# Graph attention on one core: factors of the rows in PSUM, scores of the tile two ahead behind the unit's sum

## The chip, the core and the metric

The kernel runs on one NeuronCore of a Trainium2 chip. Five engines work side by side, each in the order of its own queue: PE (matrix products), DVE (vector work), ACT (activation functions and copies), POOL (here: issues the gathers) and SP (issues the other DMAs). They wait for one another through semaphores. SBUF is the working memory of 128 partitions; [...] The metric is the time of one execution in microseconds (us); the median of several runs counts.

## The reference, cut to what matters

Two layers stand one after the other, each with a residual and a layer norm. Layer 0 is one graph attention of 8 heads over a graph of 4096 nodes with 512 features; layer 1 is an attention of 8 heads, then one of a single head of 512, then two dense layers. An attention is

```
Wh   = einsum('nf,kfp->knp', x, W)            # projection, 8 heads of 64
e    = leaky_relu(f2[:, :, None] + f1[:, None, :], 0.2)
e    = where(adj > 0, e, -1e16)
att  = softmax(e, axis=-1)                    # over a node's neighbours
out  = einsum('knm,kmp->knp', att, Wh)
```

and layer 0 is `x = layernorm(x + attention(x))`. The adjacency is sparse and skewed: low-numbered nodes have many neighbours.

## The kernel before, in words

A first stage finds every node's neighbours from the adjacency, packs them into lists of 128 edges (chunks), and projects x into a table in HBM. After that come two layers of 8 heads (`heads_layer`, called for `st0` and `st1`), and at the end the layer of one head with the dense layers. This case is about `heads_layer`.

**Tiles and units.** The 4096 nodes are 32 tiles of 128. Tile 0, whose nodes have neighbours nearly everywhere, is worked densely and spread over the whole layer (class `First`). The other 31 tiles go through their edge lists. A tile's chunks are cut into units of at most 6 chunks; a layer has 56 units, and a loop `for i, u in enumerate(units)` writes out the order of the work by hand (`manual_schedule`): each engine executes its share in just the order in which the loop names it. High and low tiles alternate, so that in the middle of the layer a tile of one unit is followed by a tile of two. A tile's first unit has `u.first` set.

**What a unit does.** `gather` (L1349, POOL) brings each chunk's 128 rows of the table to SBUF, five units ahead (`GB = 5` buffers `g`); a row has 8 heads of 64 values and, per head, one more number, the destination's part of the score. `scores` (L1441 to L1446) adds the source's part `s`, applies the leaky ReLU and writes z; ACT puts exp(z), the factor for the denominator, into the row itself (L1446). `powers` (L1455) has ACT write the same exponentials as `wp`, the factors, one number per chunk and head. `scale` first builds 0/1 matrices `sm` that tell which node an edge belongs to (L1506), then multiplies the rows by the factors (L1525, DVE, 128 x 512 numbers per chunk, here called the product). `sum` (L1547, PE) adds up the edges of each node in PSUM (`acc`). The call `weights` is `scores` and `powers` in one.

**After a tile.** Once a tile's sums are complete, `divide` divides by the denominator (L1554, L1566), adds the residual and starts the layer norm (layer 0) or the ELU (layer 1); its rest is L1671 to L1674, or L1657. Then `norm` transposes the result on PE (`pt`, L714), `project` makes the next layer's projection (`ph`, L726), `rows` copies it out on ACT (L753, L760) and writes the table, and `split` cuts the source's scores into three bf16 parts on DVE (L766 on). One step is taken per unit, so that a tile goes through them over some four units. `divide` is done early (`held`) in units that add for tile 0.

**Scores of the source.** Edges need their node's score `s`, which `Attention.spread` brings about for the tile two ahead: PE multiplies 0/1 matrices by the three bf16 parts into `pss` (L1370, L1377), and DVE collects the three into `s` and a scaled `ls` (L1386, L1398). Before, the matmuls come first in a tile's first unit, and the collection last in it.

**Tile 0.** `First.make` has ACT compute 8 blocks of weights (L1609) and scale the rows of one neighbour tile by a factor per head (L1611); `sort_out` masks the weights on DVE (L1619); `add` sums two tiles on PE (L1633, 32 products recorded as one stretch of 3.7 us); `take` adds that to a total on DVE (L1647). Each is spread over the units.

**PSUM.** `acc` takes four banks (two buffers of two banks), `pss` one, and the three others are a ring with the tag `ph`, for projections, transposes and small products. The factors `wp` lie in SBUF, with two buffers: ACT can write a unit's factors while the unit before still uses its own. A tile in a ring is handed out again once its last reader is done, and whoever writes it next waits for that.

Of the kernel before, what the change touches and what calls it, by code (L numbers as in the profile page):

```python
# [11 lines left out]
F32 = mybir.dt.float32  # L12
# [4 lines left out]
AF = mybir.ActivationFunctionType  # L17
# [5 lines left out]
P = 128  # L23
N = 4096
F = 512
NT = N // P
# [12 lines left out]
HS = 8  # L39
DM = 64  # L40
HN = P // 2
GC = 6
# [518 lines left out]
def sparse_path(  # L561
# [24 lines left out]
    nc = tc.nc  # L586
# [49 lines left out]
    class Stage2:  # L636
        def __init__(self, name, heads, dim, dest_first):
            self.name, self.heads, self.dim, self.dest_first = name, heads, dim, dest_first


            self.row = F + heads if heads > 1 else F + 2
            self.part = HF + heads // 2
            self.wide = HF + heads
            self.table = dram.tile([N + 1, self.row], F32, name=f"table_{name}")
            self.s = lists_.tile([P, NT, heads], F32, name=f"ss_{name}")
            self.s3 = lists_.tile([P, NT, 2, 3, heads], BF16, name=f"s3_{name}")
            self.s_row = None if heads > 1 else const.tile([P, 1, P], F32, name="s_row_1")
            self.rd = const.tile([P, NT, heads], F32, name=f"rd_{name}")
            self.xparts = lists_.tile([P, FC, NT], F32, name=f"xparts_{name}")
# [682 lines left out]
    class Attention:  # L1332


        def __init__(self, st, gp, wk, pacc, ps, sb=None):
            self.st, self.gp, self.wk, self.pacc, self.ps, self.sb = st, gp, wk, pacc, ps, sb
            self.s, self.ls, self.acc, self.seen = {}, {}, {}, {}

        def gather(self, u):
# [18 lines left out]
        def spread(self, t):  # L1358


            st, hs = self.st, self.st.heads
            base, n = parts_of(t)[0].first, sum(p.n for p in parts_of(t))
            for name, of in (("s", self.s), ("ls", self.ls)):
                of[t] = self.sb.tile([P, WIDE, hs], F32, name=f"{name}{hs}", tag=name, bufs=3)[:, :n]

            def scores(p, lo):

                pss = self.ps.tile([P, 20, 3, hs], F32, name="pss")
                m = min(20, p.n - lo)
                nc.tensor.matmul(  # L1370
                    pss[:, :m], ident_b,
                    hole[:, p.first + lo : p.first + lo + m, :, None].to_broadcast([P, m, 3, hs]),
                    start=True, stop=False,
                )
                todo = blocks_in(p, lo, m)
                for block, groups, chunks in todo:
                    nc.tensor.matmul(  # L1377
                        pss[:, chunks].rearrange("p m a h -> p m (a h)"),
                        s1[:, ts(p.at + block, P)],
                        st.s3[:, t, groups].rearrange("p g a h -> p g (a h)"),  # L1380
                        start=False, stop=(block, groups, chunks) == todo[-1],
                    )
                return p.first - base + lo, pss[:, :m]

            def collect(lo, pss):
                nc.vector.tensor_reduce(  # L1386
                    self.s[t][:, lo : lo + pss.shape[1]], pss.rearrange("p m a h -> p m h a"), AX.X, OP.add
                )
# [12 lines left out]

            return rest
# [46 lines left out]
        def powers(self, u):  # L1449
            if u.t == 0:  # L1450
                return
            hs, z = self.st.heads, u.z
            if hs > 1:
                u.wp = self.wk.tile([P, GC, hs], F32, name="wp", bufs=2)
                nc.scalar.activation(u.wp[:, : u.n], z, AF.Exp)  # L1455
            else:
                u.w = self.wk.tile([P, GC, hs], F32, name="w")
                nc.scalar.activation(u.w[:, : u.n], z, AF.Exp)  # L1458
# [119 lines left out]
    class First:  # L1578
# [16 lines left out]
        def make(self, step=0):  # L1595

            b = self.made
            self.step = step
            if b == min(self.summed + DW, NT) or step - self.since[b] < REST:
                return  # L1600
            self.made += 1
            rows = by_head(self.rows[b])
            d = rows[:, :, DM]
            d8 = self.sb.tile([P, HS], F32, name="d8", bufs=2)
            w = self.w[b] = self.sb.tile([P, HS, P], F32, name="w0", bufs=DW)
            nc.scalar.activation(d8, d, AF.Copy, scale=0.8)
            nc.scalar.activation(d, d, AF.Exp, scale=0.2)
            for h in range(HS):
                nc.scalar.activation(w[:, h], self.st.s_row[:, h], AF.Exp, scale=0.8, bias=d8[:, h : h + 1])  # L1609
            for h in range(HS):  # L1610
                nc.scalar.activation(rows[:, h, :DM], rows[:, h, :DM], AF.Copy, scale=rows[:, h, DM : DM + 1])  # L1611

        def sort_out(self):
            b = self.sorted
# [63 lines left out]
    def heads_layer(gp, wk, sb, pp, st, nxt, fetch, finish, clear):  # L1678
# [5 lines left out]
        order = [t for pair in zip(range(NT - 1, NT // 2, -1), many) for t in pair] + [1]  # L1684
        assert sorted(order) == list(range(1, NT))
        units = units_of(order)
        units[-1:] = units[-1].cut(units[-1].n - 2)
        groups = [(1, 1), (2, 6), (8, 8), (16, 8), (24, 8)]
        with tc.tile_pool(name=f"ha_{st.name}", bufs=2, space=PSUM, reuse_waits="tile") as pacc, \
                tc.tile_pool(name=f"hp_{st.name}", bufs=1, space=PSUM, reuse_waits="tile") as one, \  # L1690
                tc.tile_pool(name=f"hq_{st.name}", bufs=3, space=PSUM, reuse_waits="tile") as ps, \
                tc.manual_schedule():
            at = Attention(st, gp, wk, pacc, one, whole)
            extra = {}
            if clear:
                for _ in range(GB):
# [2 lines left out]
            first = First(at, whole, pacc, order[:-1] + [0, 1])  # L1699
# [3 lines left out]
            for t in order[:2]:  # L1703
                extra[t] = fetch(t)
            for _ in range(DW):
                first.make()
                first.sort_out()
            first.add(DW)
            first.take()
# [42 lines left out]
            def run(of):  # L1752

                mine = [way for way in ways if way[0] is of]
                for way in ([w for w in mine if w[1] != 0] or mine)[:1]:
                    ways.remove(way)
                    nxt_ = of(*way[1:])
                    if nxt_:
                        ways.append(nxt_)

            ways, out_, resting = [], set(), None
            for i, u in enumerate(units):
                pos = order.index(u.t)
                spread = None
                if u.first and pos + 2 < NT - 1:
                    spread = at.spread(order[pos + 2])
                    extra[order[pos + 2]] = fetch(order[pos + 2])
                if i + 1 < len(units):
                    at.weights(units[i + 1])
                taken = u.first and first.sorted - first.summed >= min(DB, NT - first.summed) > 0  # L1770
                if i > 0:
                    first.make(i)
                run(rows)
                held = None
                at.scale(u)
                first.take()
                if taken:
                    first.add(DB)
                    held = divide(order[pos - 1]) if pos > 0 else None
                    if first.summed == NT:  # L1780
                        extra[0] = fetch(0, spare())
                        resting = i + 2
                at.sum(u)
                if i + GB < len(units):
                    at.gather(units[i + GB])
                run(project)
                if first.sorted < first.made - 1 or first.made == NT:
                    first.sort_out()
                run(split)
                run(row)  # L1790
                if i == len(units) - 2:
                    assert all(way[0] is split for way in ways)
                    mrow = mean_of_all_but(pp, ps, nxt, u.t)
                run(norm)
                if held:
                    ways.append(held)
                elif u.first and pos > 0:
                    ways.append((divide, order[pos - 1]))
                    run(divide)
                if i == resting:  # L1800
                    ways.append(divide_first())
                if spread:
                    spread()
            assert resting and resting < len(units) - 4
            ways.append((divide, order[-1]))
            while ways:
# [89 lines left out]
    wk = ctx.enter_context(tc.tile_pool(name="lw", bufs=3, reuse_waits="tile"))  # L1896
# [32 lines left out]
    with tc.tile_pool(name="ta", bufs=2, space=PSUM, reuse_waits="tile") as pacc, \  # L1929
# [9 lines left out]
        order = [t for block in blocks for t in block]  # L1939
# [380 lines left out]
```

## Time and profile before

Three runs gave a median of 2035.86 us (2034.43 to 2037.29). The profiled execution took longer, as the table shows.

| What | us |
|---|---|
| median of the runs | 2035.86 |
| profiled execution | 2050.6 |
| its span, first to last instruction | 2048.9 |
| first stage, to the first gather at | 320.0 |
| layer 0, products L1525 | 353.0 to 809.0 |
| layer 1, products L1525 | 847.6 to 1305.3 |
| busy over the span: PE | 1656.7 (81%) |
| DVE | 1361.1 (66%) |
| POOL | 1192.1 (58%) |
| ACT | 902.7 (44%) |

The granted PE clock is 0.907 of full speed over the span. A line of the profile names an engine, a kernel line, the operation, what it writes and reads, and then its count, its busy time and the mean time of one instruction. The waits view names an instruction, what released it, and the total, the number and the longest of such waits. In a timeline the first two numbers are the start from the beginning of the span and the time taken, both in us; what stands in brackets is the idle time of the engine before the instruction, and what ended it. Each fp32 product on PE shows as two records. Shares over the whole span mix stages with different limits, so the layers have to be looked at by themselves. POOL's spans are rough, and the issuing of a DMA isn't counted as busy.

### The profile page before, as it was taken

How to read it: one execution, taken by the hardware profiler on the slowest of the kernel's cores; microseconds unless marked ns; L12 is line 12 of the kernel's file. 1: busy time of each engine (PE TensorE's matmuls, PEld its weight loads, DVE VectorE, ACT ScalarE, POOL GpSimd, SP SyncE). 2: the span in 40 equal slices, each digit the busy share in tenths (PEclk: the TensorE clock that was granted, in tenths of full speed). 3: DMA queues.
4: the chain of work that ended last, by engine and by line, in shares of the span. 5: the costliest groups of instructions: out<-in, count | busy, mean ns of one | idle time of the engine just before them, and what ended most of it. 6: DMA issues, size and time to landing. Idle time of an engine off the chain costs nothing.

```text
span 2048.9 us, 31053 instructions
## 1 busy us (share of the span) xinstructions
PE 1656.7 (81%) x9793; PEld 1214.9 (59%) x9793; DVE 1361.1 (66%) x3527; ACT 902.7 (44%) x3288; POOL 1192.1 (58%) x1337
## 2 busy tenths in 40 slices
PE   5997975888887887378777888658899998988987
PEld 2675654555665655256556665436668776766766
DVE  6686765978888776377666676325565656666665
ACT  5986964654555525166545563112123221212211
POOL 5556566888888781688888868173332545445100
PEclk7999996889899989689989999879999999999998
DMA  8798955666666672555565556263355444345210
GB/s 316 294 343 279 318 180 175 179 196 200 179 214 201 194 218 72 139 152 166 159 168 163 161 138 176 89 205 110 99 149 160 130 129 136 108 134 140 66 42 33
DMA packets 140052, 343.69 MB, mean 168 GB/s; under 512 B 39493, under 2 KB 44621, under 8 KB 132198
## 3 DMA queue, kind: packets, MB, share of 16 engines
q0 software_dynamic: 64064, 180.85, 32.0%
q1 hardware_dynamic: 75814, 160.76, 22.7%
q8 instruction: 80, 1.31, 0.3%
q14 instruction: 94, 0.77, 0.1%
HBM read 332.19 MB, written 42.24 MB: 183 GB/s over the span
## 4 chain that ended last, share of the span: by engine, by line
PE 33%; DVE 20%; issue 16%; POOL 9%; DMA 6%; ACT 6%; another core or an unknown queue 1%; POOLq 0%; DVEq 0%; SPq 0%; ACTq 0%
PE acc L1547 10%; POOL g L1349 8%; PE ph L726 6%; DVE g L1525 6%; DMA g<-table_t,idx 6%; PE px L2051 3%; PE acc L1633 2%; PE px L2059 2%; PE py L2051 2%; PE pz L2051 2%; PE py L2059 1%; DVE sm L1506 1%; DVE w L1619 1%; ACT sg L976 1%
## 5 line engine op out<-in xcount | busy, mean ns | idle before, releaser
L1349 POOL DMA_INDIRECT g<-table_t,idx x774 | 1007.1, 1301 | 555.6 <-issue 214.6
L1547 PE MATMUL acc<-g,sm 128*64 128x260 f32 (+2 forms) x3408 | 510.0, 439 | 253.8 <-DVE g L1525 142.8
L1547 PEld LDWEIGHTS acc<-g,sm 128*64 128x64 f32 x3408 | 281.8, 155 | 433.1 <-DVE g L1525 152.0
L726 PE MATMUL ph<-sw_t,xt 128*128 128x264 f32 (+1 forms) x1536 | 379.6, 399 | 12.5 <-ACT xt L1842 6.0
L726 PEld LDWEIGHTS ph<-sw_t,xt 128*128 128x128 f32 x1536 | 292.1, 195 | 97.4 <-issue 23.8
L1525 DVE TENSOR_TENSOR g<-g,wp 128x3072 f32<-128x3072 f32 (+4 forms) x112 | 292.5, 2611 | 0.0
L717 ACT ACTIVATE xt<-pt 128x128 f32<-128x128 f32 x256 | 67.4, 277 | 276.2 <-PE pt L714 188.2
L1609 ACT ACTIVATE w<-s_row,d 128x128 f32<-128x128 f32 x512 | 156.3, 387 | 0.0
L1633 PE MATMUL acc<-rows,w 128*128 128x65 f32 x1024 | 129.0, 287 | 14.7 <-DVE w L1619 14.7
L1633 PEld LDWEIGHTS acc<-rows,w 128*128 128x128 f32 x1024 | 125.1, 203 | 16.5 <-issue 16.5
L1157 DVE MAX8 cand<-key 128x8 f32<-128x85 f32 (+51 forms) x395 | 99.9, 318 | 47.2 <-PE key L991 47.1
L1611 ACT ACTIVATE rows<-rows 128x64 f32<-128x64 f32 x512 | 128.4, 334 | 0.0
L976 ACT ACTIVATE sg<-raw,value 128x2048 bf16<-128x2048 int32 x60 | 120.1, 2008 | 3.6 <-DMA raw<-in_adj_dram 2.9
L1441 DVE TENSOR_TENSOR z<-s,g 128x16 f32<-128x16 f32 (+5 forms) x160 | 29.9, 201 | 129.2 <-DMA g<-table_t,idx 125.1
L2065 ACT ACTIVATE shid<-shid,sl1b 128x256 f32<-128x256 f32 x112 | 50.5, 500 | 117.0 <-DVE shid L2003 115.2
L1657 DVE SCALAR_TENSOR_TENSOR o<-ex,o 128x512 f32<-128x512 f32 x63 | 43.5, 690 | 63.4 <-ACT ex L1656 50.1
L1666 ACT ACTIVATE rstd<-mv,s_eps 128x1 f32<-128x1 f32 x64 | 19.1, 298 | 150.2 <-DVE mv L1663 143.1
L1619 DVE SCALAR_TENSOR_TENSOR w<-w,mask 128x1024 f32<-128x1024 f32 x64 | 77.4, 1212 | 5.2 <-ACT w L1609 5.2
L753 ACT COPY hrow<-ph 128x260 f32<-128x260 f32 (+3 forms) x130 | 44.1, 369 | 70.8 <-PE ph L726 61.0
L1655 ACT ACTIVATE ex<-o 128x512 f32<-128x512 f32 x63 | 39.8, 631 | 77.6 <-DVE o L1573 57.8
L1446 ACT ACTIVATE g<-z 128x48 f32<-128x48 f32 (+4 forms) x112 | 30.3, 271 | 90.9 <-DVE z L1444 60.0
L1514 DVE TENSOR_SCALAR sm<-iota_n,nl,w 128x64 f32<-128x64 f32 x284 | 68.9, 319 | 0.2 <-ACT w L1458 0.2
(282 smaller groups left out, 2813.4 us busy)
## 6 DMA issues: line engine op xcount, KB each, us to landing
raw<-in_adj_dram SPq DMA_DIRECT2D x60, 1024.0 KB
table_t<-hrow SPq DMA_DIRECT2D x64, 260.0 KB
rows<-table_t SPq DMA_DIRECT2D x64, 260.0 KB
xr<-in_x_dram SPq DMA_DIRECT2D x63, 256.0 KB
g<-table_t,idx POOLq DMA_INDIRECT x774
table_t<-hrow SPq DMA_DIRECT2D x32, 257.0 KB
xr<-sx_d SPq DMA_DIRECT2D x32, 256.0 KB
out_dram<-xr SPq DMA_DIRECT2D x32, 256.0 KB
```

The source lines that it names most:

```text
L726: nc.tensor.matmul(ph[:n], columns(c), st.w[:, c, j], start=(c == 0), stop=(c == FC - 1))
L976: nc.scalar.activation(sg[:, ts(i, w)], raw[:, ts(i, w)], AF.Sign, bias=values["half"])
L1157: nc.vector.max(out=cand[:, at : at + 8], in_=key[:, j - w0_ : j - w0_ + n_])
L1349: nc.gpsimd.indirect_dma_start(out=u.g[:, k, : self.st.row], out_offset=None, in_=self.st.table[:, :], in_offset=bass.IndirectOffsetOnAxis ...
L1514: nc.vector.tensor_scalar(sm[:, at + i], of_g, node[k], u.w[:, k], op0=OP.is_equal, op1=OP.mult)
L1525: nc.vector.tensor_mul(body, body, wp[:, :, None].to_broadcast(body.shape))
L1547: nc.tensor.matmul(out_[g * HN : (g + 1) * HN], sm[:, slot], rows(k), start=start, stop=stop)
L1609: nc.scalar.activation(w[:, h], self.st.s_row[:, h], AF.Exp, scale=0.8, bias=d8[:, h : h + 1])
L1611: nc.scalar.activation(rows[:, h, :DM], rows[:, h, :DM], AF.Copy, scale=rows[:, h, DM : DM + 1])
L1619: nc.vector.scalar_tensor_tensor(w, w, 1.0, mask0[:, self.turns[b], None, :].to_broadcast([P, HS, P]), op0=OP.max, op1=OP.mult)
L1633: nc.tensor.matmul(acc[:, j, k * HD : (k + 1) * HD], w[:, h], rows[:, h * HD : (h + 1) * HD], start=(b == lo and k == 0), stop=(b == hi - ...
L2051: nc.tensor.matmul(out_[:, m], a[:, c, ts(k, P)], b[:, c], start=m == 0 and c == 0, stop=k == ks[-1] and c == 1,)
```

## The change

It touches the two layers of 8 heads in four places.

- `wp` moves from SBUF, with two buffers, to one bank of PSUM, with one buffer. That is the bank that `pss` had.
- `pss` takes its turns in the ring of three banks that projections and transposes use (`tag="ph"`).
- In each unit, `scores` and `powers` are called apart. `run(rows)` comes directly after `scores`; then tile 0's exponentials; then `powers`; then tile 0's scaling of rows, which `make` now hands back as a function.
- `spread` is called after the unit's `sum` and the next gather, before `project`, and its collection directly after `sort_out`, ahead of `split`, `row`, `norm` and `divide`. Before, it was called at the start of the unit and the collection came at the end.

The number of products, activations, DMAs and gathers in a unit stays as it is. Its core as a diff:

```diff
-        def __init__(self, st, gp, wk, pacc, ps, sb=None):
+        def __init__(self, st, gp, wk, pacc, ps, sb=None, one=None):
...
-                pss = self.ps.tile([P, 20, 3, hs], F32, name="pss")
+                pss = self.ps.tile([P, 20, 3, hs], F32, name="pss", tag="ph")
...
-                u.wp = self.wk.tile([P, GC, hs], F32, name="wp", bufs=2)
+                u.wp = self.one.tile([P, GC, hs], F32, name="wp")
...
-            for h in range(HS):
-                nc.scalar.activation(rows[:, h, :DM], rows[:, h, :DM], AF.Copy, scale=rows[:, h, DM : DM + 1])
+
+            def scale_rows():
+                for h in range(HS):
+                    nc.scalar.activation(rows[:, h, :DM], rows[:, h, :DM], AF.Copy, scale=rows[:, h, DM : DM + 1])
+
+            return scale_rows
...
-            at = Attention(st, gp, wk, pacc, one, whole)
+            at = Attention(st, gp, wk, pacc, ps, whole, one)
...
-                first.make()
+                first.make()()
...
                 pos = order.index(u.t)
-                spread = None
                 if u.first and pos + 2 < NT - 1:
-                    spread = at.spread(order[pos + 2])
                     extra[order[pos + 2]] = fetch(order[pos + 2])
                 if i + 1 < len(units):
-                    at.weights(units[i + 1])
+                    at.scores(units[i + 1])
                 taken = u.first and first.sorted - first.summed >= min(DB, NT - first.summed) > 0
-                if i > 0:
-                    first.make(i)
                 run(rows)
+                scale_rows = first.make(i) if i > 0 else None
+                if i + 1 < len(units):
+                    at.powers(units[i + 1])
+                if scale_rows:
+                    scale_rows()
                 held = None
                 at.scale(u)
                 first.take()
...
                 at.sum(u)
                 if i + GB < len(units):
                     at.gather(units[i + GB])
+                spread = at.spread(order[pos + 2]) if u.first and pos + 2 < NT - 1 else None
                 run(project)
                 if first.sorted < first.made - 1 or first.made == NT:
                     first.sort_out()
+                if spread:
+                    spread()
                 run(split)
                 run(row)
...
                 if i == resting:
                     ways.append(divide_first())
-                if spread:
-                    spread()
```

More of the change, by code (lines that the diff above doesn't have):

```diff
@@ L1332, in sparse_path @@
     class Attention:
-        def __init__(self, st, gp, wk, pacc, ps, sb=None):
-            self.st, self.gp, self.wk, self.pacc, self.ps, self.sb = st, gp, wk, pacc, ps, sb
+        def __init__(self, st, gp, wk, pacc, ps, sb=None, one=None):
+            self.one, self.st, self.gp, self.wk, self.pacc, self.ps, self.sb = one, st, gp, wk, pacc, ps, sb
             self.s, self.ls, self.acc, self.seen = {}, {}, {}, {}
@@ L1599, in make @@
             if b == min(self.summed + DW, NT) or step - self.since[b] < REST:
-                return
+                return None
             self.made += 1
```

## The prediction

> **What bounds the kernel now.** I read the busy time by stretch first, for the middle of each layer of 8 heads: the columns are the stretch and its length, then busy us and instruction counts of PE, PE's weight loads, DVE, ACT and POOL, then PE's clock, the DMA share and GB/s.
>
> ```profile
> 445.00:681.00 236.00, 189.14 (x1280) 138.66 (x1280) 196.71 (x405) 123.81 (x592) 193.88 (x136) 0.90 0.67 204
> 947.00:1187.00 240.00, 189.59 (x1272) 138.50 (x1273) 163.07 (x300) 136.07 (x592) 197.63 (x136) 0.89 0.59 163
> ```
>
> POOL has 136 gathers in either stretch. Each is followed by 0.30 us of issue, so POOL is taken for 193.9 + 40.8 = 234.7 of 236 us and 238.4 of 240. No other engine is over 83%. The gathers set the pace of both layers. Then the timeline, all engines, beside one product of rows and factors (L1525):
>
> ```profile
> 515.26 1.00 POOL L1349 DMA_INDIRECT g<-table_t,idx  x1 [0.30 <-issue]
> ...
> 516.32 3.35 DVE L1525 TENSOR_TENSOR g<-g,wp 128x3072 f32<-128x3072 f32 x1
> 516.57 3.97 POOL L1349 DMA_INDIRECT g<-table_t,idx  x1 [0.30 <-issue]
> ```
>
> A gather takes 1.00 us; one that begins under the product takes 3.97 and ends 0.87 us after it (519.67 to 520.54). Laying each gather's excess over 1.0 us to the DVE instruction that covers most of it gives L1525 93 us in layer 0 and 94 in layer 1, other DVE work 17 and 13. Last, what ends DVE's waits in layer 0 (345 to 825) and layer 1 (845 to 1320):
>
> ```profile
> DVE z L1441 <- DMA g<-table_t,idx: 27.3, 15, 4.7
> ```
>
> ```profile
> DVE z L1441 <- DMA g<-table_t,idx: 84.7, 32, 4.7
> ```
>
> So late gathers cost DVE much in layer 1 and little in layer 0, where DVE itself is the next to be full.
>
> [...] (L1566 reads PSUM in 692 ns, L1916 adds the same size from SBUF in 692). [...] 16 product records of L1547 take 3.46 us after 4.61 us idle, 1.97 after 1.99.
>
> **The change, part by part.** (1) Factors in PSUM. 112 ACT writes (226 ns) and 112 products (2302 ns at the middle) stay. Removed: POOL's 93 + 94 = 187 us of blocking[...]. POOL then needs about 186 of the 236 us and falls behind DVE and PE. At factor instructions I take 0[...]. (2) One buffer for the factors: ACT waits for the product, up to 0.7 + 3.4 us after the scores. Queued behind it are the 8 row scalings (2.0 us), needed a unit or more later, and work that itself waits for DVE instructions after the product. ACT is half idle (124 of 236): 0; exposed by 1 us in a third of the units it is +37. (3) Rows' copies (L753) ahead of tile 0's 10 exponentials and 8 scalings: they were up to 4.7 us behind them. DVE's split of s (L766) waited 6.3 us at 691 and 8.9 at 1199 for just that: -9 in all, half in each layer. (4) The scores of tile two ahead: their matmuls went first in the unit's PE work and DVE collected at its end. Now PE does them after the unit's own sum (L1547), and DVE collects right after sorting, ahead of the normalization's rest and of the next unit's product. DVE is in order, so this adds a wait: DVE stands at the collection until PE has done product -> sum -> scores of the same unit, and all that PE had queued before. Nothing else in the diff adds instructions: same matmuls, DMAs and queues; the ring's banks come free well before their turn (a projection's copies end units earlier).
>
> **The price of part 4.** Three units (two tiles) make a period in the middle: first unit d of one tile with tile 0's sum before it, first unit e of the next tile, its second unit f. Timeline of DVE and of PE, layer 0:
>
> ```profile
> 606.10 0.30 DVE L1386 TENSOR_REDUCE s<-pss 128x48 f32<-128x144 f32 x1
> ...
> 607.61 2.28 DVE L1525 TENSOR_TENSOR g<-g,wp 128x2048 f32<-128x2048 f32 x1
> ...
> 610.41 0.15 DVE L1671 SCALAR_TENSOR_TENSOR rstd<-mv,rstd 128x1 f32<-128x1 f32 x1
> ```
>
> ```profile
> 603.00 3.77 PE L1633 MATMUL acc<-rows,w 128*128 128x65 f32 x32
> 606.70 3.72 PE L1547 MATMUL acc<-g,sm 128*64 128x260 f32 x28
> 610.35 3.83 PE L726 MATMUL ph<-sw_t,xt 128*128 128x264 f32 x16
> 614.01 0.27 PE L1370 MATMUL pss<-hole,s_identb 128*128 128x240 bf16 x1
> 614.12 0.30 PE L1377 MATMUL pss<-s_t,s 128*128 128x48 bf16 x6
> 614.35 1.98 PE L1547 MATMUL acc<-g,sm 128*64 128x260 f32 x16
> ```
>
> The reader is to see that DVE collected at 606.10, before d's sum had begun at 606.70. After the change the loop closes: PE's f sum 1.90, projection 3.67, transposes 0.43, tile 0's sum 3.70, d's sum 2.85, scores 0.41 (starts to starts) = 12.96; DVE from d's collection to the end of e's product 3.79; PE e's sum and scores 2.31; DVE from e's collection over rest and division 0.60 + 3.64, scores and product of f 3.35 = 7.59; four handoffs 0.25. Sum 26.9 us in layer 0. In layer 1 rest and division take 1.54 instead of 3.64 (1116.04 to 1117.58): 24.8. PE waits some 5 us before f's sum, so that sum runs cold: up to +1.5, I take half. Units are often longer (12 to 16 slots instead of 8: +0.24 us a slot pair on PE, +0.5 to 1.1 on DVE). Doing this for the nine periods from the twelfth to the fortieth unit gives 266 us in layer 0 and 247 in layer 1, against 244.5 (436.9 to 681.4, ends of the two products) and 248.6 (938.7 to 1187.3) now: +22 and -1. The first twelve units are worked likewise. There first units follow each other, each with a collection behind its sum: layer 0's first product ends at 355.8, its sum runs cold for 4.3, scores 0.5, collection 0.5, then 4.6 to the end of the second product, 365.7 where it is 360.9 now. To the twelfth product that makes +6 in layer 0; in layer 1 the shorter rest and division and the gathers' share in today's 88.2 us turn it to -6. From the fortieth to the fifty-third product (100.4 and 98.7 us now) two units of one tile follow two of the next and half the units collect; DVE's own work (7.4 us a unit in layer 0) is already nearly the whole pace there, and with part 3's gain I get -2, and -8 in layer 1, where gathers set it. Elsewhere nothing changes. Stalls that POOL's pace now hides (DVE's "remote" waits: 7.9 and 5.6 us) fall on the loop: +7. Sum: +26 - 15 + 7 = +18. The profiled execution took 2050.6 us (span 2048.9), so about 2067 there; the median of the runs is 2035.9 (0.7% lower), so **2054**.
>
> **Rivals.** (a) The relief wins, 0.22: PE runs so little behind DVE that sum and scores of d (3.3 us) end within DVE's division and sorting (3.6 us), and the collections cost nothing. For it: at several units the sum starts 0.1 us after its product. Against: tile 0's sum stands before d's. Without the waits at d and e (3.4 and 1.9 us a period) a period is DVE's 22.5 us of work, some 24 in practice: 9 x (2.2 + 2.7) = -44, with the ends' gains about -50: 1985. It decides where a period falls under 26.2 (layer 0) and 26.7 (layer 1). (b) Factors in PSUM don't free POOL, 0.14: gathers still stretch to 4 us, the loop is added to POOL's pace where they don't overlap: layer 1 loses its -15 and gains some 13 instead, +39 with layer 0's 26: 2075. (c) ACT's wait is exposed, 0.12: +37 as in part 2: 2090.
>
> **From this the numbers.** Forecast 0.52 (its own range 2032 to 2078, of which 0.06 falls within 0.2% and 0.04 below). A measurement here tells about 0.2%. Faster: 0.04 + 0.21 = 0.25; within 0.2%: 0.06 + 0.01 + 0.01 = 0.08; slower 0.67. Leaving out the far half of (a) and of (c) gives 2000 to 2095.
>
> **What would show it.** Right: gathers at 1.0 us under L1525 and POOL idle in the middle stretches; DVE's waits for gathers nearly gone, replaced by waits at L1386 for PE's scores, some 5 us a period; PE waiting for L1525 before second units; layer 0 longer, layer 1 about equal or shorter. Wrong: L1386 without waits (a), gathers still at 3 to 4 us (b), DVE products waiting for ACT's L1455 (c).

## The result, and the profile after

The changed kernel takes 2114.92 us (median of 6 runs, 2111.53 to 2117.07) where the kernel before took 2032.78 (6 runs, 2025.5 to 2037.29): **1.0404 times as long, interval 1.0381 to 1.0426**. The forecast was 2054 with a range to 2095; slower was right, but the change costs 82 us where the sum gave 18, and the time lies 61 us over the forecast. Below, DVE's and PE's lines of the helper functions have moved by a few: tile 0's sum is L1637, its total L1651, the normalization's rest L1675 to L1678.

First the busy time by stretch. The stretches here are those from the end of the twelfth to that of the fortieth product in each layer, with the same columns as before: PE, weight loads, DVE, ACT, POOL, then PE's clock, the DMA share and GB/s. These 28 products took 244.5 and 248.6 us before.

```profile
453.60:738.80 285.20, 200.93 (x1301) 145.19 (x1300) 202.13 (x418) 131.49 (x614) 133.78 (x131) 0.84 0.56 169
1002.80:1267.40 264.60, 200.88 (x1300) 145.44 (x1299) 167.31 (x310) 142.63 (x613) 136.53 (x131) 0.85 0.54 146
```

POOL, which had been taken for 99% of the middle of both layers, now works 133.8 + 131 x 0.30 = 173 us of 285 and 176 of 265. PE is at 70 and 76%, DVE at 71 and 63%. No engine is full: the layers have become a chain of waits. The timeline of the changed kernel beside a product shows why POOL is free:

```profile
657.58 1.00 POOL L1349 DMA_INDIRECT g<-table_t,idx  x1 [0.30 <-issue]
657.83 2.28 DVE L1525 TENSOR_TENSOR g<-g,wp 128x2048 f32<-128x2048 f32 x1
...
658.88 1.00 POOL L1349 DMA_INDIRECT g<-table_t,idx  x1 [0.31 <-issue]
```

The gather that starts at 658.88, in the middle of the product, takes 1.00 us, where its like took 3.97. The excess over 1.0 us that was laid to L1525, 93 and 94 us, is 0.7 in either layer. Now what ended DVE's waits, from the page's and the groups' lines of L1386 (busy and mean, then idle time before it), first in the kernel before, then in the changed one:

```profile
L1386 DVE TENSOR_REDUCE s<-pss 128x48 f32<-128x144 f32 (+3 forms) x64 | 22.3, 348 | 36.3 <-remote 13.5 <-PE pss L1377 12.7 <-PE pt L714 5.7
```

```profile
L1386 DVE TENSOR_REDUCE s<-pss 128x48 f32<-128x144 f32 (+3 forms) x64 | 22.8, 358 | 231.9 <-PE pss L1377 231.9
```

The same in the waits view of the changed kernel, where the layers end later: layer 0 (345 to 860), then layer 1 (880 to 1395):

```profile
DVE s L1386 <- PE pss L1377: 103.7, 28, 6.4
DVE g L1525 <- ACT wp L1455: 14.0, 3, 5.3
```

```profile
DVE s L1386 <- PE pss L1377: 128.2, 29, 9.5
DVE z L1441 <- DMA g<-table_t,idx: 17.1, 3, 10.2
DVE g L1525 <- ACT wp L1455: 13.5, 3, 5.8
```

Waits for gathers went from 27.3 and 84.7 us to next to none and 17.1; waits for the spread scores came in their place, over twice as long. In the stretches above they are 70.0 and 89.0 us, 7.8 and 9.9 a period of three units. A second new wait is smaller: three products a layer stand for their factors.

One period of three units in the middle of layer 0, PE first, then DVE. It has the same units as the period that the prediction shows.

```profile
652.29 3.72 PE L1547 MATMUL acc<-g,sm 128*64 128x260 f32 x28
655.94 0.24 PE L1370 MATMUL pss<-hole,s_identb 128*128 128x144 bf16 x1
...
660.81 1.97 PE L1547 MATMUL acc<-g,sm 128*64 128x260 f32 x16 [0.88 <-PE ph L726]
...
670.89 3.58 PE L1547 MATMUL acc<-g,sm 128*64 128x260 f32 x16 [5.23 <-DVE g L1525]
674.40 3.83 PE L726 MATMUL ph<-sw_t,xt 128*128 128x264 f32 x16
678.07 0.60 PE L714 MATMUL pt<-s_ident,o 128*128 128x128 f32 x4
678.50 3.69 PE L1637 MATMUL acc<-rows,w 128*128 128x65 f32 x32
```

```profile
656.32 0.31 DVE L1386 TENSOR_REDUCE s<-pss 128x48 f32<-128x144 f32 x1 [5.79 <-PE pss L1377]
...
657.83 2.28 DVE L1525 TENSOR_TENSOR g<-g,wp 128x2048 f32<-128x2048 f32 x1
660.02 0.68 DVE L1651 TENSOR_TENSOR total<-total,acc 128x520 f32<-128x520 f32 x1
663.17 0.41 DVE L1386 TENSOR_REDUCE s<-pss 128x80 f32<-128x240 f32 x1 [2.46 <-PE pss L1377]
...
668.56 2.28 DVE L1525 TENSOR_TENSOR g<-g,wp 128x2048 f32<-128x2048 f32 x1
```

The two engines take turns. DVE stands 5.79 us until PE has done sum and scores. PE then has a projection to do and stands 0.88 us for DVE's product and total; DVE stands 2.46 us for the next sum and scores, and PE 5.23 us for the next product. One turn of the loop, from tile 0's sum at 648.67 to the next at 678.50, takes 29.8 us, where the prediction summed up 26.9. Three numbers make the difference. The prediction's sum has 2.85 us for d's sum (L1547); that of the period shown takes 3.65, here (652.29 to 655.94) as in the prediction's own timeline (606.70 to 610.35). The last sum of the period is cold, as it is called here: the granted clock over it is 0.53 of full speed, about half, and it takes 3.58 us. The sum of as many records at 660.81 is warm, with a clock of 1.00, and takes 1.97. The prediction has 1.90 in the 26.9 and names the cold beside it. And the sum at 660.81 starts 0.7 us after its product ended: it starts when DVE's total (660.02 to 660.70) has freed the accumulator. 26.9 + 0.8 + 1.6 + 0.7 gives 30.0.

### The profile page after: what moved, and what is told of

The parts are those of the page before. It is cut to its first block, busy times and chain, and to the rows that moved or that the text cites. A ratio compares the mean times of both kernels' runs of the same rounds, so it can differ in the third digit from the quotient of the medians.

```text
span 2114.5 us, 31069 instructions
## 1 busy us (share of the span) xinstructions
PE 1677.3 (79%) x9773; PEld 1228.9 (58%) x9793; DVE 1356.7 (64%) x3527; ACT 909.1 (43%) x3288; POOL 992.8 (47%) x1337
## 4 chain that ended last, share of the span: by engine, by line
PE 39%; DVE 14%; issue 8%; POOL 4%; DMA 4%; ACT 2%; POOLq 0%; DVEq 0%; SPq 0%; ACTq 0%
PE acc L1547 14%; PE ph L726 7%; DVE g L1525 4%; POOL g L1349 4%; PE acc L1637 4%; DMA g<-table_t,idx 3%; PE px L2057 3%; PE px L2065 2%; PE py L2057 2%; PE pz L2057 1%; PE py L2065 1%; PE acc L1477 1%; DVE sm L1506 1%; PE pz L2065 1%; DVE xr L2009 1%
## 5 line engine op out<-in xcount | busy, mean ns | idle before, releaser
L1349 POOL DMA_INDIRECT g<-table_t,idx x774 | 807.8, 1044 | 817.7 <-PE acc L1547 367.8
L1547 PE MATMUL acc<-g,sm 128*64 128x260 f32 (+2 forms) x3408 | 528.0, 452 | 276.4 <-DVE g L1525 146.1
L1547 PEld LDWEIGHTS acc<-g,sm 128*64 128x64 f32 x3408 | 294.8, 160 | 464.6 <-DVE g L1525 159.1
L726 PE MATMUL ph<-sw_t,xt 128*128 128x264 f32 (+1 forms) x1536 | 375.0, 396 | 6.6 <-ACT xt L1848 5.7
L1525 DVE TENSOR_TENSOR g<-g,wp 128x3072 f32<-128x3072 f32 (+4 forms) x112 | 291.6, 2604 | 27.4 <-ACT wp L1455 27.4
L717 ACT ACTIVATE xt<-pt 128x128 f32<-128x128 f32 x256 | 67.2, 277 | 314.5 <-PE pt L714 314.5
L1386 DVE TENSOR_REDUCE s<-pss 128x48 f32<-128x144 f32 (+3 forms) x64 | 22.8, 358 | 231.9 <-PE pss L1377 231.9
L1637 PE MATMUL acc<-rows,w 128*128 128x65 f32 x1024 | 127.0, 286 | 17.7 <-DVE w L1623 14.7
L1637 PEld LDWEIGHTS acc<-rows,w 128*128 128x128 f32 x1024 | 125.8, 204 | 20.0 <-issue 19.6
L714 PE MATMUL pt<-s_ident,o 128*128 128x128 f32 x248 | 41.7, 294 | 46.8 <-DVE rd_t L1554 29.4
L1661 DVE SCALAR_TENSOR_TENSOR o<-ex,o 128x512 f32<-128x512 f32 x63 | 43.4, 689 | 51.5 <-ACT ex L1660 51.5
```

What stands on the lines that cost most here:

```text
L726: nc.tensor.matmul(ph[:n], columns(c), st.w[:, c, j], start=(c == 0), stop=(c == FC - 1))
L1349: nc.gpsimd.indirect_dma_start(out=u.g[:, k, : self.st.row], out_offset=None, in_=self.st.table[:, :], in_offset=bass.IndirectOffsetOnAxis ...
L1525: nc.vector.tensor_mul(body, body, wp[:, :, None].to_broadcast(body.shape))
L1547: nc.tensor.matmul(out_[g * HN : (g + 1) * HN], sm[:, slot], rows(k), start=start, stop=stop)
L1637: nc.tensor.matmul(acc[:, j, k * HD : (k + 1) * HD], w[:, h], rows[:, h * HD : (h + 1) * HD], start=(b == lo and k == 0), stop=(b == hi - ...
```

## The experiments

Every ratio is to the kernel before, timed beside the run in question; it needed between 2032.78 and 2057.32 us on these occasions, so times in us are only compared within one. The theory is the loop: DVE stands at the collection for PE's product -> sum -> scores, and PE for DVE's product. The rivals: the one factor bank, the shared ring, or ACT's order cost the time.

### Parts undone one at a time

**The scores back in their old place** (computed first in the unit, collected last), the rest as changed:

```diff
+                spread = None
                 if u.first and pos + 2 < NT - 1:
+                    spread = at.spread(order[pos + 2])
                     extra[order[pos + 2]] = fetch(order[pos + 2])
...
-                spread = at.spread(order[pos + 2]) if u.first and pos + 2 < NT - 1 else None
...
-                if spread:
-                    spread()
                 run(split)
...
                     ways.append(divide_first())
+                if spread:
+                    spread()
```

> The changed kernel with one part undone: the scores of tile two ahead are computed at the start of the first unit and collected at its end, as in the kernel before; factors in one PSUM bank, the shared ring of three banks and the order of rows' copies, powers and row scalings stay. Theory (the loop PE sum, scores, DVE collection is what costs): DVE's 232 us of waits at L1386 shrink to under 40, and as POOL stays free (gathers 1.0 us under L1525) the time falls below the kernel before: 1975 to 2015, best guess 1995. Rival (the one factor bank or the ring costs, wherever the scores are): waits move to other instructions and the time stays at 2090 to 2120. Rival (DVE's own work is the pace of layer 0): 2020 to 2040, no better than before.

Measured: 1.0263 (1.0206 to 1.0321). The waits at the collection fell from 231.9 to 65.5 us, and still the kernel stayed slower than before. By this run alone the loop would seem a third of the matter. The groups (L1370 in the kernel before, then in this one) and PE's timeline of this kernel show what came instead:

```profile
L1370 PE MATMUL pss<-hole,s_identb 128*128 128x144 bf16 (+3 forms) x64 | 16.2, 253 | 11.9 <-issue 6.3 <-DVE s L1386 4.7 <-DVE bs L1661 1.0
```

```profile
L1370 PE MATMUL pss<-hole,s_identb 128*128 128x144 bf16 (+3 forms) x64 | 16.5, 261 | 67.7 <-issue 47.8 <-ACT xt L717 19.9
```

```profile
521.06 0.28 PE L1370 MATMUL pss<-hole,s_identb 128*128 128x144 bf16 x1 [2.53 <-ACT xt L717]
521.13 0.32 PE L1377 MATMUL pss<-s_t,s 128*128 128x48 bf16 x3
521.28 7.07 PE L1637 MATMUL acc<-rows,w 128*128 128x65 f32 x32
528.28 4.25 PE L1547 MATMUL acc<-g,sm 128*64 128x260 f32 x24
```

First in the unit, `pss` finds no free bank in the ring: PE stands 67.7 us at L1370 (11.9 in the kernel before, where `pss` had its own bank). The view puts only 19.9 of them down to ACT's copies of the transposes (L717), but each of the 18 waits ends 0.05 us after the last of such copies. The work behind these waits is slow: tile 0's sum takes 7.07 us here instead of 3.69. Over all, L1637 is busy for 168.7 us where the changed kernel needs 127.0. So this run exchanges one new wait for another: the old place and the ring don't go together. The ring was in the first rival, but that rival had it cost time wherever the scores are, and this run can't tell that.

**The move of the scores alone, on the kernel before**; factors in SBUF, `pss` in a bank of its own:

```diff
-                spread = None
                 if u.first and pos + 2 < NT - 1:
-                    spread = at.spread(order[pos + 2])
...
                     at.gather(units[i + GB])
+                spread = at.spread(order[pos + 2]) if u.first and pos + 2 < NT - 1 else None
...
                     first.sort_out()
+                if spread:
+                    spread()
...
                     ways.append(divide_first())
-                if spread:
-                    spread()
```

> The kernel before with one part of the change alone: the scores of tile two ahead behind the unit's own sum and collected right after the sorting. Factors stay in SBUF with two buffers, the scores in a bank of their own, exponentials and row scalings in their old order. Theory (the loop costs): slower than before by most of what the change costs, and POOL's stretched gathers (3.97 us under L1525) still stand beside it: 2090 to 2130. Rival (what costs is the one factor bank): no slower than 2050. If it is well above 2130, the relief of POOL was worth something in the changed kernel.

Measured: 1.0524 (1.0478 to 1.0571), worse than the whole change. Its line of L1386:

```profile
L1386 DVE TENSOR_REDUCE s<-pss 128x48 f32<-128x144 f32 (+3 forms) x64 | 23.0, 359 | 278.6 <-PE pss L1377 241.7 <-PE ph L726 22.2 <-PE acc L1547 6.5
```

At 2033 us for the kernel before this would be 2140, above the 2130 expected. One part makes more than all of the loss, without ring or factor bank; the other parts take 1.2% off it (1.0524 to 1.0404).

**The collection back at the end of the unit**, the scores still behind the sum:

```diff
-                if spread:
-                    spread()
                 run(split)
...
                     ways.append(divide_first())
+                if spread:
+                    spread()
```

> The changed kernel, but DVE collects the scores at the end of the first unit, after the normalization's rest and the division, as in the kernel before; PE still computes them behind the unit's sum. Theory: the loop keeps its PE part, but DVE does its 3.6 us of division and rest before it waits for the scores, and PE's next sum waits only for scores and product after the collection: the period falls from 29.9 to about 26, 2 layers x 9 periods x 3.6 = 65 us at most: 2030 to 2070. Rival (it is the matmuls' place behind the sum alone that costs): within 10 us of the changed kernel, 2105 to 2125.

Measured: 1.0279 (1.0223 to 1.0335), between what theory and rival gave; the waits at L1386 are still 205.5 us. DVE does its division before it waits, which shortens the loop, but the scores still come after the sum.

**The factors back in two SBUF buffers**, the rest as changed:

```diff
-                u.wp = self.one.tile([P, GC, hs], F32, name="wp")
+                u.wp = self.wk.tile([P, GC, hs], F32, name="wp", bufs=2)
```

> The changed kernel with the factors back in two SBUF buffers; all else as changed. Theory (loop sets the pace, POOL's blocking comes back but is partly under it; the 27.5 us of DVE waiting for the factors, L1525 behind L1455, come from ACT's order and stay): 2110 to 2150, gathers again at 3 to 4 us under L1525. Rival (the one factor bank is what costs, ACT's wait for the product before it): 2050 to 2090, and ACT's 42 us of waits for L1525 and DVE's waits for L1455 are gone.

Measured: 1.0503 (1.0456 to 1.055). The gathers of the changed kernel, then of this one:

```profile
L1349 POOL DMA_INDIRECT g<-table_t,idx x774 | 807.8, 1044 | 817.7 <-PE acc L1547 367.8 <-issue 195.5 <-PE pss L1377 112.1
```

```profile
L1349 POOL DMA_INDIRECT g<-table_t,idx x774 | 967.2, 1250 | 706.1 <-PE acc L1547 311.4 <-issue 206.2 <-PE pss L1377 58.6
```

Their mean goes from 1044 to 1250 ns. Taken as a whole, the move of the factors is no cause of the loss: without it the kernel is another 1.0% slower. This run brings back two buffers and POOL's blocking together, so it doesn't price the single bank by itself. The relief of POOL is thus real, but with the loop in place it is worth only this 1.0%.

### The scores ahead of the sum

The direct test of the loop. The matmuls of the scores go ahead of the unit's own sum, so that DVE's collection needs only PE's earlier work. The ring, the factor bank, ACT's order and the collection's place stay as changed.

```diff
+                spread = at.spread(order[pos + 2]) if u.first and pos + 2 < NT - 1 else None
                 at.sum(u)
                 if i + GB < len(units):
                     at.gather(units[i + GB])
-                spread = at.spread(order[pos + 2]) if u.first and pos + 2 < NT - 1 else None
```

> The changed kernel, with the matmuls of the spread scores just ahead of the unit's own sum (behind tile 0's sum) instead of behind it; DVE's collection stays where the change put it. Theory (DVE stands at the collection for PE's product -> sum -> scores): the unit's own sum (2.3 to 3.7 us) leaves the loop twice a period, which then falls from 29.9 to about 25 us in layer 0, bound by DVE; L1386's waits fall from 232 to under 90 us and the time to 0.985 to 1.01 of the kernel before. Rival (the run with the scores in their old place lost the collections' waits and stayed at 1.026, as the factors' bank and the ring took over): L1386's waits fall, those of L1525 for ACT's L1455 rise over 50 us, and the ratio is 1.02 to 1.035.

Measured: **0.9722 (0.9687 to 0.9758)**, below what the theory gave. PE's timeline of this kernel, and its line of L1386:

```profile
571.39 3.68 PE L1637 MATMUL acc<-rows,w 128*128 128x65 f32 x32
574.91 0.23 PE L1370 MATMUL pss<-hole,s_identb 128*128 128x144 bf16 x1
574.97 0.25 PE L1377 MATMUL pss<-s_t,s 128*128 128x48 bf16 x4
575.15 2.85 PE L1547 MATMUL acc<-g,sm 128*64 128x260 f32 x24
```

```profile
L1386 DVE TENSOR_REDUCE s<-pss 128x48 f32<-128x144 f32 (+3 forms) x64 | 22.6, 356 | 93.3 <-PE pss L1377 93.2
```

Half a microsecond of matmuls moved across a sum of 2 to 3.7 us, and 6.8% of the time of the kernel before is gone (1.0404 to 0.9722). The stretch from the twelfth to the fortieth product falls from 285.2 to 245.5 us in layer 0 and from 264.6 to 216.1 in layer 1. The loop is shown, and the ring is cleared for this place of the scores.

**The powers right behind the scores on ACT**, on the changed kernel: `at.weights(units[i + 1])` in place of `at.scores`, and the later `at.powers` gone. **And both edits together.**

> The changed kernel with the powers (L1455) right behind the unit's scores on ACT, as before, ahead of the rows' copies and of tile 0's exponentials. Theory (the product's 27.5 us of waits for the factors come from ACT's order, the powers behind copies that wait for PE): these waits go, and half to all of them is gained: ratio 1.026 to 1.034. Rival 1 (the loop refills the time): 1.036 to 1.044. Rival 2 (ACT now waits for the product before the rows' copies, and these come late for PE and SP): 1.045 or more, with waits of PE for L753 and of DVE for L760.

> Both edits: scores just ahead of the unit's own sum, powers right behind the unit's scores. Theory of the loop with the factors' waits as second term: L1386 under 90 us and L1525's waits for L1455 under 15, so the relief of POOL is left alone: ratio 0.97 to 0.995. Rival (something else of the change costs: the ring, PE at half clock after its waits): 1.005 or more.

Measured: 1.0422 (1.0381 to 1.0464) and 0.9719 (0.9682 to 0.9756), each the same as without the edit. The groups of the first:

```profile
L1386 DVE TENSOR_REDUCE s<-pss 128x48 f32<-128x144 f32 (+3 forms) x64 | 22.8, 358 | 253.8 <-PE pss L1377 253.8
L1525 DVE TENSOR_TENSOR g<-g,wp 128x3072 f32<-128x3072 f32 (+4 forms) x112 | 291.6, 2604 | 8.9 <-ACT wp L1455 8.9
```

The waits for factors fell from 27.4 to 8.9 us, and those for scores rose by 21.9. The factors' waits are plain to see in the profile, and taking most of them away gains nothing, as the waits for scores take up the time.

**Both edits, and the collection at the end of the unit:**

> As the run with both edits, and the collection at the end of the unit as in the kernel before. Theory: DVE's division and normalization lie between, so L1386's waits are under 30 us; another 0 to 1% faster than with the collection early: ratio 0.965 to 0.99. Rival (the collection ends late, so that the next product and PE's ring wait for it): slower than with the collection early, above 0.995.

Measured: **0.9519 (0.9478 to 0.9561)**, 1934.78 us beside 2034.36: the fastest of all. L1386 waits 65.1 us, more than the 30 expected. The same kernel once more:

> Repeat look at the version with the scores ahead of the sum, the powers early and the collection at the end, on this chip, as the base for the next two runs. Expected as measured: 0.952 of the kernel before.

Measured: 1935.18 us in a single execution, again 0.952 of the kernel before. In this kernel, the factors were then put back into SBUF, with the same diff as above:

> The version with the scores ahead of the unit's sum, powers early and collection at the end (0.952 of the kernel before), with one part undone: the factors in two SBUF buffers. Theory (with the loop gone, the relief of POOL is what is left of the change's gain): gathers stretch to 4 us under L1525 again, POOL sets the pace as in the kernel before, and DVE's waits for gathers (L1441) come back: ratio 0.985 to 1.01. Rival (the gain comes from the order of ACT or the place of the scores, not from POOL): ratio 0.95 to 0.965.

Measured: 0.9994 (0.9981 to 1.0007), as slow as the kernel before, and POOL has its old load again. The groups of the fastest version, then of this one:

```profile
L1349 POOL DMA_INDIRECT g<-table_t,idx x774 | 818.6, 1058 | 623.1 <-PE acc L1547 270.9 <-issue 209.1 <-DMA table_t<-mrow 56.6
```

```profile
L1349 POOL DMA_INDIRECT g<-table_t,idx x774 | 1010.4, 1305 | 525.3 <-issue 208.1 <-PE acc L1547 184.8 <-DMA rows<-table_t 50.4
L1441 DVE TENSOR_TENSOR z<-s,g 128x16 f32<-128x16 f32 (+5 forms) x160 | 30.2, 201 | 148.5 <-DMA g<-table_t,idx 148.0 <-issue 0.3
```

So one edit, factors in PSUM, is worth 1.0% with the loop (1.0503 to 1.0404) and 4.8% with the loop opened (0.9994 to 0.9519). And the new order without the relief is worth nothing: POOL sets the pace.

**The scores ahead of tile 0's sum too**, in the fastest version: the call of `at.spread` goes ahead of `if taken:`, behind which tile 0's sum is called.

> The fastest version so far (scores ahead of the unit's sum, powers early, collection at the end; 0.952) with the scores' matmuls ahead of tile 0's sum too. Theory (what is left of L1386's waits, 65 us, is PE's work queued ahead of the scores): 3.7 us of PE work less ahead of them in half of the units, L1386 under 30 us, ratio 0.935 to 0.948. Rival (the ring: the bank comes free only when ACT has copied the rows, so PE waits at L1370 as it did with the scores in their old place): PE waits at L1370 grow over 30 us, ratio above 0.955.

Measured: 0.9546 (0.9514 to 0.9578), no gain, as the intervals overlap. L1386's waits fell to 33.9 us, close to the 30 of the theory, but the time didn't follow; PE's waits at L1370 grew only to 22.2 us, 11.1 a layer, less than the rival needed. Neither holds. Layer 0's middle got 4 us shorter and layer 1's 9 us longer, where DVE waits more for the ELU's results on ACT (L1661: 22.8 us instead of 12.2 between 800 and 1290) and for the copies of `s` (L766: 21.0 instead of 14.5). That these waits are the cause was not tested.

### The terms that the loop's sum lacked

**Tile 0's total ahead of the collection**, where DVE stands anyway:

```diff
                 if spread:
+                    first.take()
                     spread()
```

> The changed kernel, but DVE adds tile 0's sum to its total (L1651, 0.7 us) just ahead of the collection, where DVE stands waiting anyway, instead of behind the next unit's product. Theory (0.7 us of the loop that the prediction left out: the next tile's sum on PE needs the accumulator that this add frees): about 9 + 4 periods a layer, 0.7 us each: 15 to 20 us less than the changed kernel, ratio 1.031 to 1.034. Rival (the add is covered by other waits in the loop): within 5 us of it, ratio 1.038 to 1.043.

Measured: 1.0308 (1.0287 to 1.033), 19.5 us less than the changed kernel by the ratios (0.0096 x 2033). The middle stretches lose 5.3 and 7.8 us. In the trace the sum of all 18 such units e in the two stretches starts 0.1 us after its product, where it was 0.7 to 0.9. The term is as large as expected.

**PE kept warm**: extra matmuls in PE's wait ahead of a second unit's sum, into accumulator columns that nobody reads. They add work and leave the result alone.

```diff
+                if not u.first:
+                    for _ in range(12):
+                        nc.tensor.matmul(
+                            at.acc[u.t][:, 1, 264:F], ident, nxt.w[:, 0, 0, : F - 264], start=False, stop=False
+                        )
                 at.sum(u)
```

> The changed kernel with 12 extra matmuls[...] on PE ahead of the sum of each second unit, into accumulator columns that nobody reads; they only fill PE's wait for the product, and leave the result as it is. Theory (PE's sum of a second unit runs at half clock after the 5 us wait, 41.0 us for ten units of layer 0 where 25 is the time of warm ones, and this lengthens every period): these sums take 2.0 us for 8 slots instead of 3.7, and the loop gains up to 1.6 us a period: 20 to 35 us less than the changed kernel, ratio 1.023 to 1.031. Rival (the cold sum is covered elsewhere): 1.037 to 1.043. If the extra matmuls themselves come late: 1.045 or more.

Measured: 1.0724 (1.0703 to 1.0744): the last case of the expectation. Twelve of them took 6.5 to 7.5 us, and second units all over the layers had to stand for them; nothing follows on the cold sums. With six, and only in the units of the middle stretches (`12 <= i < 40`):

> The changed kernel with 6 extra matmuls instead of 12, and only ahead of the second units' sums between the twelfth and the fortieth unit, where PE waits some 5 us. In the run with 12 they took 6.5 to 7.5 us[...], ended up to 3 us after the product, and the sums behind them took 1.98 instead of 3.7 us for 8 slots. With 6 they should end before the product. Theory (the cold sums lengthen the loop by 1.6 us a period): 10 units a layer, 1.6 us each: 25 to 32 us less than the changed kernel, ratio 1.025 to 1.029. Rival (the loop is as long with warm sums, as something else ends at the same time): 1.037 to 1.043. If the sums are still cold, nothing follows.

Measured: 1.0338 (1.0316 to 1.0361). PE's timeline of this kernel, at the same place as the period shown above:

```profile
655.78 4.36 PE L1790 MATMUL acc<-sw_t,s_ident 128*128 128x248 f32 x12
661.20 1.97 PE L1547 MATMUL acc<-g,sm 128*64 128x260 f32 x16 [1.05 <-DVE g L1525]
```

The six matmuls show as twelve records. The sum takes 1.97 us instead of 3.58. Over the ten second units of a stretch the sums take 28.1 instead of 41.0 us in layer 0 (two of them stayed cold), 25.0 instead of 42.3 in layer 1, and the stretches are 10.8 and 10.0 us shorter. By the ratios the kernel gains 13.4 us (0.0066 x 2033), half of what was expected. A kernel with 65 us of useless matmuls is faster than one without: that shows that the cold sums are a term of the loop.

**The rows' copies first, alone, on the kernel before** (part 3 of the prediction):

```diff
+                run(rows)
                 if i > 0:
                     first.make(i)
-                run(rows)
```

> The kernel before with one part alone: the rows' copies (L753) ahead of tile 0's exponentials and scalings. Forecast of the prediction: DVE's waits at the split of s for L760 (15.7 and 17.8 us) shrink, 9 us in all, ratio 0.9955. Rival (gathers on POOL are the pace, the waits are slack): 0.998 to 1.002, with the split's waits shrunk and those for gathers grown.

Measured: 0.9989 (0.9971 to 1.0008), no difference that can be told. The waits for L760 fell from 33.5 to 13.4 us, by more than the 9 of the forecast, and those for gathers rose from 125.1 to 160.1: slack, as the rival said.

## Why the prediction was right or wrong

**Right: part 1, what is removed.** The gathers' 187 us of excess under the product are down to 1.3, and the product with a PSUM input costs nothing more (mean 2604 against 2611 ns). Rival (b) is out. That factors in PSUM would free POOL was the author's assumption, as the kernel before has no such product; the gathers at 1.00 us under it are the first to show it. That one edit is worth 4.8% once the loop is opened, where rival (a) had -50 us (2.5%) for the whole change.

**Right: the mechanism of part 4.** DVE's wait at L1386 took the place of its waits for gathers, PE waits for the product ahead of second units, and the direction of the whole follows. The runs with the scores ahead of the sum show it as the cause. The size of the waits was not right: 7.8 and 9.9 us a period instead of some 5; and layer 1, told as about equal or shorter, is 16 us longer in its middle.

**Wrong: the price of part 4.** The step that failed is the sum of the loop, 26.9 us a period in layer 0 and 24.8 in layer 1, and with it 266 and 247 us for the middle stretches, which took 285.2 and 264.6. That is 37 us of the miss; the first twelve units are about 20, those from the fortieth on about 8. (That is 65; the forecast had 7 us for stalls beside these stretches, and the last three products of the layers took 3 us more, which leaves the 61.)

Two terms are measured. DVE's total between e's product and e's sum, 0.7 us, was left out, as the sum followed only who reads `g` and not who frees the accumulator; 13 us in these stretches, 19.5 in the whole kernel. And "up to +1.5, I take half" for f's cold sum: the sums of the ten second units of layer 0 take 41.0 us, warm ones 25, so the cold costs 1.6 us each. But warm sums won back only 13 to 21 us in both layers, of which the forecast had counted 13.5; so at most 8 us of the miss are this.

The rest, 16 to 24 us of the 37, is not settled. Cold sums of first units fit, 4.9 and 6.9 us in the two layers: counted from 0 as in the loop, those of units 12, 19 and 28, and in layer 1 of 22 too (granted clock 0.50 to 0.62; 3.74 instead of 1.97 us for unit 12). With the scores ahead of the sum, all records of L1547 are busy for 505.9 us instead of 528.0. But this is read from the traces, and no run tested it alone. The 2.85 us for d's sum, 0.8 too little in the period shown, may be a part as well; the prediction doesn't say what it took for d in the other periods.

**Wrong: the first twelve units** were put at +6 and -6 and took +18 and +1.4; with the scores ahead of the sum they take 83.2 and 77.3 us instead of 99.4 and 89.6, so it is the same loop. The first sum of layer 0, put at 4.3 us cold, took 5.5 (354.25 to 359.72, at a granted clock of 0.50); which of its terms were short beyond that is open.

**Part 2** put the single factor buffer at nothing. Waits came (27.4 us of DVE for the factors), and taking 18.5 us of them away gained nothing. So the 0 stands here, and rival (c), which had such waits in full, is out. **Part 3** at -9 us was wrong as a price by itself in the kernel before, though its waits shrank: there DVE waits less for ACT and longer for the gathers. Inside the change it was not tested.

**Rival (a)** was priced at 1985 on the condition that the collections cost nothing. With the scores ahead of the sum, 93 of the 232 us of these waits are left, and the kernel takes 1974.63. (The periods at which it would decide, 26.2 and 26.7 us, are the stretches of 236 and 240 us divided by nine. The nine periods took 244.5 and 248.6, so 27.2 and 27.6 would have been right, and its -44 would have been -61.) The condition failed in the change itself because tile 0's sum, which the prediction names against it, and the unit's own stand ahead of the scores. The error was not in the choice between the two, but in a loop's sum put together from mostly warm durations and without the accumulator.

## What to carry to other kernels

Where two in-order engines hand work to each other both ways, put what the other engine waits for ahead of the long work, not behind it: here 0.5 us of matmuls a tile, moved across one sum, is 6.8% of the kernel. A relief is worth what the next limit leaves of it, so price the two together: the same edit gave 1.0% with the loop and 4.8% with the loop opened. And when a loop is summed, walk it by buffers as well as by data (who frees what the next step writes), and take PE's durations after a wait, not between busy neighbours (here 3.58 and 1.97 us for sums of 16 records); waits beside a loop may stand in the profile in full and still be worth nothing.

## What the runs showed of the hardware

PE's lower clock is part of such a loop: in the changed kernel, a sum of 16 records behind a wait of 5.23 us took 3.58 us at a granted clock of 0.53; one behind 0.88 us took 1.97 at 1.00. With the longer wait filled by extra matmuls, the same sum took 1.97, and the middle stretches were 10.8 and 10.0 us shorter. The wait just before doesn't settle it: of these two sums in the changed kernel, behind nearly the same idle time, the first has a granted clock of 1.00, the second of 0.62:

```profile
563.51 2.85 PE L1547 MATMUL acc<-g,sm 128*64 128x260 f32 x24 [2.15 <-issue]
...
625.63 4.54 PE L1547 MATMUL acc<-g,sm 128*64 128x260 f32 x24 [2.13 <-issue]
```

What was not expected is that matmuls for nothing pay, 1.0404 to 1.0338.

A gather that started under a product with one PSUM input took 1.00 us (one took 1.55); with both inputs in SBUF it took up to 4.13. The product itself took as long either way (mean 2604 and 2611 ns).
